# A selective-scan kernel: the middle row group interleaved by padded weights, one DMA per quad, pieces at other units, and states that enter a scan through its first token

## The chip, the cores and the metric

The kernel runs on one core of a Trainium2 chip. The metric is the device time of one execution in microseconds (us), from three runs. Before the change it is 13006.98 us at the median (13003.53 to 13008.28). Profiles are of one execution; their times count from the first instruction. The engines are TensorE (PE, with its weight loads as PEld), VectorE (DVE), ScalarE (ACT), GpSimd (POOL) and SyncE (SP), which issues the DMAs here. Each works through its own queue in order.

## The reference

The input is x of shape (2, 96, 128, 128) in float32. The model has two layers, and nearly all of the time goes into the first half of the first one: four Mamba blocks that read the normalized image as a sequence of 16384 tokens in four directions (rows, rows reversed, columns, columns reversed). Each block has 192 inner channels and 16 states per channel.

```python
xc, z = jnp.split(x @ in_w.T, 2, axis=-1)          # 96 -> 192 and 192
xc = silu(causal_conv4(xc) + conv_b)               # depthwise, 4 taps
xdbl = xc @ xproj_w.T                              # dt_raw (6), B (16), C (16)
dt = softplus(dt_raw @ dt_w.T + dt_b)
h = exp(dt * A) * h + dt * B * u                   # for each token, channel, state
y = einsum('bds,bs->bd', h, C)
y = (y + Dp * xc) * silu(z)
out = y @ outp_w.T                                 # then the fuse over 4 directions
```

After the Mamba blocks come a quantized feed-forward layer, a 3x3 convolution and a second feed-forward layer, with normalizations between. The change does not touch these.

## The kernel before

For each of the two images the kernel runs three stages one after the other: normalize (the image by rows and by columns goes to DRAM), mamba, and ffn_and_conv. Only mamba and the weights' setup change.

**Tiling.** Directions are worked on in pairs (PAIRS): a row direction and a column direction, 2 x 192 = 384 channels, in three groups g of 128 partitions. Group 0 holds channels 0 to 127 of the first direction, group 2 the last 128 of the second, and the middle group, g = 1, holds 64 of each: partitions 0 to 63 for the first direction, 64 to 127 for the second. A *step* is 512 tokens of one pair; there are 32 steps in a pair and 64 in an image. Step i = 0 of a pair starts from zero states. Within a step the states of a group are taken two at a time. Such a pair of states of one group is a *unit*: 24 units in a step, units 0 to 7 of group 0, 8 to 15 of group 1, 16 to 23 of group 2.

**A unit's work.** ACT computes the decay exp(dt * A) for the two states into PSUM (`decay`, L330). POOL multiplies the B rows by dt * u (`b_part`, L324). DVE runs two scans over the 512 tokens (`scan`, L334), one for each state, with the recurrence's multiply and add in one instruction, and then multiplies the states by the C rows (L409). PE adds these products into the output y by matmuls with the identity (`sums`, L341). ACT copies the last states into `hst` (L410); the scan of the same unit in the next step takes them as its initial value. When a group's eight units are done, DVE multiplies y with the gate (`gated`, L349), PE starts the next group's y with the skip term (L416), and `project` and `collect` bring two groups at a time into the result (L357 to L365).

**Rows.** B and C are the same for all channels of a direction, so each step writes its 64 rows to DRAM in four copies (`rows_out`, L261, four DMAs) and reads them back onto 128 partitions, four states at once, a *quad* of 1 MB that serves two units (`row_tile`, L320). For the middle group a quad comes by two DMAs, each to 64 partitions.

**Order.** All engine queues are written out by hand. The loop runs over the units of all steps. In unit k it issues, in this order: the fetch of a B quad (every second unit, for unit k + 6), POOL's `b_part` for unit k + 2, pieces due at (k, 0), the first scan of unit k, everything behind unit k - 1 (product, state copy, gated product, sums), the second scan of unit k, the fetch of a C quad (for k + 4), ACT's decay for unit k + 2, and pieces due at (k, 1).

**Pieces.** The next step's input work is spread over the units of this one, at the places in the table `at` (L301 to L310): loading the input (`load`), three convolutions (`conv`, `conv_out`; the four taps are folded into the weights, L207 and L233), three gate projections (`gate`, `gate_out`), two `silu` passes with a table load before and after (L244, L245), the projection to B, C and dt (`rows`, `rows_out`), and for each group seven pieces that make dt by a softplus (`dt_in` on PE; `dt_exp`, `dt_ln` on ACT; `dt_q`, `dt_log`, `dt_sum`, `dt_u` on POOL). Convolutions, gates, rows, dt_in and project share one PSUM buffer, `misc`, so that each waits until ACT has read the one before. For the middle group `inproj` issues, for each tap, two matmuls of 64 output rows, one from each direction.

**Setup.** Weights are loaded once; the convolution's input weights are multiplied by their taps (L97), and the output projection is folded with the fuse weights into `gmat` (L112).

Of the kernel before, what the change touches and what calls it, by code (L numbers as in the profile page):

```python
# [42 lines left out]
def tile_metaformer(ctx: ExitStack, tc: tile.TileContext, a: dict, out: bass.AP):  # L43
# [22 lines left out]
    inz = const("inz", (C, 4, DI))  # L66
# [11 lines left out]
    inx = cpool.tile([C, 4, 4, DI], F32, name="inx")  # L78
    nc.vector.memset(gmat, 0.0)
    with tc.tile_pool(name="prep", bufs=1) as pp, tc.tile_pool(name="prep_ps", bufs=2, space=PSUM) as pps:  # L80
# [11 lines left out]
        inxw = pp.tile([C, 4, DI], F32, name="inxw")  # L92
        nc.sync.dma_start(inxw, a["inx"])
        taps = pp.tile([C, 4, 4, DI], F32, name="taps")
        nc.sync.dma_start(taps, a["taps"].broadcast_to((C, 4, 4, DI)))
        for d in range(4):
            nc.vector.tensor_tensor(inx[:, d], taps[:, d], inxw[:, d, None, :].broadcast_to((C, 4, DI)), ALU.mult)  # L97
        outw = pp.tile([C, 4, DI], F32, name="outw")
        nc.sync.dma_start(outw, a["outw"])
        fusew = pp.tile([C, 4, C], F32, name="fusew")  # L100
        nc.sync.dma_start(fusew, a["fusew"])
        for pi, (da, db) in enumerate(PAIRS):

            pieces = [
                (slice(0, 128), da, 0, 128),
                (slice(0, 64), da, 128, 192),
                (slice(64, 128), db, 0, 64),
                (slice(0, 128), db, 64, 192),
            ]
            for g, (rows, d, lo, hi) in enumerate(pieces):  # L110
                ps = pps.tile([128, C], F32, name="ps")
                nc.tensor.matmul(ps[rows, :], outw[:, d, lo:hi], fusew[:, d, :], start=True, stop=True)  # L112
                nc.vector.tensor_copy(gmat[rows, pi, g, :], ps[rows, :])
# [69 lines left out]
    def mamba(acc, xnr, xnc):  # L183

        with ExitStack() as st:
# [5 lines left out]
            hst = one.tile([128, NG, S], F32, name="hst")  # L191
            acc_w = acc.rearrange("c (h w) -> c w h", w=W)
# [4 lines left out]
            def inproj(pi, g, w, src, taps):  # L197

                ps = misc()
                for k in taps:  # L200
                    se = {"start": k == taps[0], "stop": k == taps[-1]}
                    for d, rows, lo, hi in (
                        ((0, slice(0, 128), 0, 128),),
                        ((0, slice(0, 64), 128, 192), (1, slice(64, 128), 0, 64)),
                        ((1, slice(0, 128), 64, 192),),
                    )[g]:
                        nc.tensor.matmul(ps[rows, :], w(PAIRS[pi][d], k, lo, hi), src[d][:, k : k + T], **se)  # L207
                return ps

            def prologue(pi, i, d):  # L210
# [16 lines left out]
                def conv(g):  # L227
                    d["ps"] = inproj(pi, g, lambda dd, k, lo, hi: inx[:, dd, k, lo:hi], src, (0, 1, 2, 3))
# [6 lines left out]
                def gate(g):  # L235
                    d["ps"] = inproj(pi, g, lambda dd, k, lo, hi: inz[:, dd, lo:hi], src, (3,))
# [18 lines left out]
                def rows_out():  # L255

                    d["rows"] = one.tile([BCO + NBC, T], F32, name="rows")
                    nc.scalar.copy(d["rows"], d["ps"][0 : BCO + NBC, :])
                    d["bcd"] = rows_d.tile([COPIES, 2, NBC // 2, T], F32, name="bcd")
                    for n in range(COPIES):  # L260
                        nc.sync.dma_start(d["bcd"][n].rearrange("k r t -> (k r) t"), d["rows"][BCO:, :])  # L261
# [38 lines left out]

                at = [(0, 0, load), (8, 1, partial(silu, "xc")), (14, 1, partial(silu, "sz"))]  # L301
                at += [(12, 0, rows), (12, 1, rows_out)]
                for g, k in enumerate((4, 5, 6)):
                    at += [(k, 0, partial(conv, g)), (k, 1, partial(conv_out, g))]
                for g, k in enumerate((7, 10, 11)):
                    at += [(k, 0, partial(gate, g)), (k, 1, partial(gate_out, g))]
# [129 lines left out]
            for k in range(total + 6):  # L436
# [4 lines left out]
                if k % 2 == 0:  # L441
                    fetch(k + 2 * B_AHEAD, 0, B_AHEAD, bs)
# [180 lines left out]
```

## Time and profile before

| What | Value |
|---|---|
| Time, median of three runs | 13006.98 us |
| Profiled execution | 13004.29 us |
| Its span, first to last instruction | 13002.5 us |
| DVE busy | 11569.1 us, 89% |
| PE busy | 10850.3 us, 83% |
| POOL busy | 9215.4 us, 71% |
| ACT busy | 8560.0 us, 66% |
| DMA queue q1, share of 16 engines | 83.1%, 3394.12 MB |
| POOL's waits for rows (L324) | 1419.2 us |
| DVE's waits for rows (L409) | 18.8 us |
| Mean granted TensorE clock | 0.963 |

Busy time is the union of an engine's instructions. A group is a set of instructions with the same line, engine, operation and tiles; its row gives the busy time, the mean duration in ns, and the idle time of the engine just before these instructions with what ended it. Instructions of DVE and POOL overlap a little at their ends, so that their pitch, from start to start, is shorter than their duration. In a timeline a row begins with its start and its length in us; a bracket gives the idle time before it and who ended it.

The two mamba stages are the stretches in which DVE is at 90% or more: from 168 to 5937 us, and from 6661 to 12427 us.

### The profile page before, as it was taken

The numbers are of one execution on the slowest core, as the hardware profiler recorded it, in microseconds if no ns is written. First come the engines' busy times: TensorE is split into PE (matmuls) and PEld (weight loads), VectorE is DVE, ScalarE is ACT, GpSimd is POOL, SyncE is SP. The second block draws the span as 40 slices with busy tenths as digits, with TensorE's granted clock in tenths as the row PEclk, the third lists the DMA queues.
The fourth block names the chain that finished last, engine by engine and source line by source line (L and its number), as shares of the span: only waits on it lengthen the run. The fifth ranks groups of instructions, "written<-read, shape, count | busy, mean of one in ns | idle before, by whom it ended". The sixth has DMA issues, their size and how long they took to land. (4 is left out here: it accounts for less than half of the span.)

```text
span 13002.5 us, 97992 instructions
## 1 busy us (share of the span) xinstructions
PE 10850.3 (83%) x24208; PEld 3987.1 (31%) x24208; DVE 11569.1 (89%) x10865; ACT 8560.0 (66%) x14738; POOL 9215.4 (71%) x4772
## 2 busy tenths in 40 slices
PE   6888888888888888888978888888888888888889
PEld 2323233333333333333323333332333333333233
DVE  5999999999999999995459999999999999999954
ACT  6666666666666666665566666666666666666655
POOL 4877778777787787772147778777787777877721
PEclk8999999999999999999989999999999999999999
DMA  7999999999999999992079999999999999999920
GB/s 226 287 294 282 298 288 285 295 283 298 288 285 295 283 295 289 285 295 68 13 226 285 298 283 292 290 285 298 285 291 291 284 298 286 290 294 281 296 61 13
DMA packets 545331, 3400.40 MB, mean 262 GB/s; under 512 B 81612, under 2 KB 82732, under 8 KB 146840
## 3 DMA queue, kind: packets, MB, share of 16 engines
q1 hardware_dynamic: 544760, 3394.12, 83.1%
q8 instruction: 195, 3.19, 0.1%
q14 instruction: 376, 3.08, 0.1%
HBM read 3288.94 MB, written 104.86 MB: 261 GB/s over the span
## 5 line engine op out<-in xcount | busy, mean ns | idle before, releaser
L324 POOL TENSOR_TENSOR row<-dtu,row 128x1024 f32<-128x1024 f32 x3072 | 7175.7, 2358 | 1739.3 <-DMA row<-bcd 1419.2
L334 DVE TENSOR_TENSOR_SCAN da<-da,hst,row 128x512 f32<-128x512 f32 x5952 | 7339.4, 1274 | 351.2 <-ACT da L330 194.6
L341 PE MATMUL y<-row,ident 128*128 128x512 f32 x12288 | 6120.1, 626 | 1113.3 <-DVE row L409 1098.9
L330 ACT ACTIVATE da<-dt,amat 128x512 f32<-128x512 f32 x6144 | 4249.4, 692 | 207.5 <-ACT hst L410 0.4
L341 PEld LDWEIGHTS y<-row,ident 128*128 128x128 f32 x12288 | 2288.9, 197 | 4779.4 <-DVE row L409 2292.3
L409 DVE TENSOR_TENSOR row<-da,row 128x1024 f32<-128x1024 f32 x3072 | 3705.9, 1206 | 19.6 <-DMA row<-bcd 18.8
L410 ACT COPY hst<-da 128x2 f32<-128x2 f32 x3072 | 484.0, 158 | 2235.5 <-DVE row L409 2233.3
L416 PE MATMUL y<-xc,dmat 128*128 128x512 f32 x768 | 526.1, 773 | 779.1 <-DVE sz L349 779.1
L287 POOL TENSOR_TENSOR q<-e,q 128x512 f32<-128x512 f32 x384 | 488.0, 1271 | 821.8 <-ACT hst L410 709.1
L233 ACT ACTIVATE xc<-misc,convb 128x512 f32<-128x512 f32 x384 | 264.2, 688 | 1117.5 <-PE misc L207 1117.5
L207 PE MATMUL misc<-xa,inx 96*128 96x512 f32 (+1 forms) x2048 | 932.4, 597 | 59.0 <-DMA xa<-xnr 57.2
L207 PE MATMUL misc<-xb,inx 96*64 96x512 f32 (+1 forms) x2048 | 928.1, 595 | 1.6 <-ACT xc L233 1.6
L531 POOL TENSOR_TENSOR acc<-acc,y 96x512 f32<-96x512 f32 x128 | 147.6, 1153 | 987.0 <-DVE y L530 987.0
L541 PE MATMUL pc<-pad,kw 96*96 96x512 f32 x1152 | 566.7, 593 | 0.0
L207 PEld LDWEIGHTS misc<-xa,inx 96*128 96x128 f32 (+1 forms) x2048 | 323.6, 163 | 625.5 <-issue 493.4
L293 POOL TENSOR_TENSOR dt<-dt,ln 128x512 f32<-128x512 f32 x384 | 486.9, 1268 | 30.1
L297 POOL TENSOR_TENSOR dtu<-dt,xc 128x512 f32<-128x512 f32 x384 | 488.5, 1272 | 0.5
L290 POOL TENSOR_TENSOR ln<-ln,q 128x512 f32<-128x512 f32 x384 | 488.1, 1271 | 0.5
L359 PE MATMUL misc<-sz,gmat 128*96 128x512 f32 x1024 | 483.6, 594 | 0.0
L416 PEld LDWEIGHTS y<-xc,dmat 128*128 128x128 f32 x768 | 129.0, 211 | 1102.1 <-DVE sz L349 1099.1
L268 PE MATMUL misc<-rows,dtw 12*128 12x512 f32 x768 | 439.7, 652 | 18.5 <-ACT dt L275 17.2
L132 DVE TENSOR_TENSOR xq<-xm,rs 96x512 fp8e5<-96x512 f32 x128 | 87.9, 687 | 387.8 <-ACT rs L128 387.8
(75 smaller groups left out, 8403.8 us busy)
## 6 DMA issues: line engine op xcount, KB each, us to landing
row<-bcd SPq DMA_DIRECT2D x2048, 1024.0 KB, 7.5
row<-bcd SPq DMA_DIRECT2D x2048, 512.0 KB, 8.0
bcd<-rows SPq DMA_DIRECT2D x512, 128.0 KB, 9.8
xa<-xnr SPq DMA_DIRECT2D x124, 193.1 KB, 5.8
xb<-xnc SPq DMA_DIRECT2D x124, 193.1 KB, 5.5
acc<-in_x_dram SPq DMA_DIRECT2D x16, 768.0 KB, 17.8
xnr<-xn SPq DMA_DIRECT2D x16, 768.0 KB, 4.3
xnc<-stg SPq DMA_DIRECT2D x16, 768.0 KB, 5.6
```

The source lines that it names most:

```text
L207: nc.tensor.matmul(ps[rows, :], w(PAIRS[pi][d], k, lo, hi), src[d][:, k : k + T], **se)
L287: nc.gpsimd.tensor_tensor(d["q"], d["e"], d["q"], ALU.subtract)
L290: nc.gpsimd.tensor_tensor(d["ln"], d["ln"], d["q"], ALU.add)
L293: nc.gpsimd.tensor_tensor(d["dt"][g], d["dt"][g], d["ln"], ALU.add)
L297: nc.gpsimd.tensor_tensor(dtu, d["dt"][g], d["xc"][:, g, :], ALU.mult)
L324: nc.gpsimd.tensor_tensor(b, d["dtu"][g][:, None, :].broadcast_to((128, 2, T)), b, ALU.mult)
L330: nc.scalar.activation(da[:, j, :], d["dt"][g], AF.Exp, scale=amat[:, pi, g, s + j : s + j + 1])
L334: nc.vector.tensor_tensor_scan(h[:, j, :], da[:, j, :], b[:, j, :], 0.0 if i == 0 else hst[:, g, s + j : s + j + 1], ALU.mult, ALU.add,)
L341: nc.tensor.matmul(y, ident, c[:, j, :], start=False, stop=s + j == S - 1)
L409: nc.vector.tensor_tensor(c, h, c, ALU.mult)
L416: nc.tensor.matmul(y, dmat[:, pi, g, :], d["xc"][:, g, :], start=True, stop=False)
L541: nc.tensor.matmul(pc, kw[:, t, :], rows, start=t == 0, stop=t == 8)
```

## The change

1. **States through the first token.** A scan's initial value is the constant 0.0. Instead, the state that enters a step is added to the first token's input: for each group ACT computes exp(dt * A) of the step's first token (128x16) and POOL multiplies it by `hst` into `enter` (`entering`, due at units 20, 28 and 36 counted from the start of the step before), and in every unit of a step with i > 0 POOL adds two columns of `enter` to the first token of the B product.
2. **The middle group's rows in turn.** Its 128 channels alternate between the two directions, partition by partition. Setup pads the weights with zero columns (`padded`), so that each of the middle group's matmuls has 128 output columns, half of them zero, and both directions accumulate into the same PSUM rows: eight matmuls in a row for a convolution, two for a gate.
3. **One DMA per quad.** With channels in turn, the copies in DRAM are laid out so that one DMA fills 128 partitions for the middle group too. The copies are written by two DMAs with a broadcast instead of four.
4. **Pieces at other units.** The table `at` changes; outputs are now one unit after the matmuls they read. Writing the rows to DRAM is a piece of its own.
5. **Setup.** The taps are loaded in four parts through one buffer, and `gmat` needs no clearing.

```diff
             hst = one.tile([128, NG, S], F32, name="hst")
+            enter = one.tile([128, NG, S], F32, name="enter")
...
-            def inproj(pi, g, w, src, taps):
+            def inproj(g, w, src, taps):
 
                 ps = misc()
-                for k in taps:
-                    se = {"start": k == taps[0], "stop": k == taps[-1]}
-                    for d, rows, lo, hi in (
-                        ((0, slice(0, 128), 0, 128),),
-                        ((0, slice(0, 64), 128, 192), (1, slice(64, 128), 0, 64)),
-                        ((1, slice(0, 128), 64, 192),),
-                    )[g]:
-                        nc.tensor.matmul(ps[rows, :], w(PAIRS[pi][d], k, lo, hi), src[d][:, k : k + T], **se)
+                parts = [(k, j) for k in taps for j in ((0,), (1, 2), (3,))[g]]
+                for n, (k, j) in enumerate(parts):
+                    nc.tensor.matmul(ps, w(k, j), src[j // 2][:, k : k + T], start=n == 0, stop=n == len(parts) - 1)
                 return ps
...
                 def rows_out():
-
                     d["rows"] = one.tile([BCO + NBC, T], F32, name="rows")
                     nc.scalar.copy(d["rows"], d["ps"][0 : BCO + NBC, :])
-                    d["bcd"] = rows_d.tile([COPIES, 2, NBC // 2, T], F32, name="bcd")
-                    for n in range(COPIES):
-                        nc.sync.dma_start(d["bcd"][n].rearrange("k r t -> (k r) t"), d["rows"][BCO:, :])
+
+                def rows_to_dram():
+
+                    d["bcd"] = rows_d.tile([2, COPIES, NBC // 2, T], F32, name="bcd")
+                    for k in range(2):
+                        r = d["rows"][BCO + k * NBC // 2 : BCO + (k + 1) * NBC // 2, None, :]
+                        r = r.broadcast_to((NBC // 2, COPIES, T))
+                        nc.sync.dma_start(d["bcd"][k].rearrange("n r t -> r n t"), r)
...
-                at = [(0, 0, load), (8, 1, partial(silu, "xc")), (14, 1, partial(silu, "sz"))]
-                at += [(12, 0, rows), (12, 1, rows_out)]
-                for g, k in enumerate((4, 5, 6)):
-                    at += [(k, 0, partial(conv, g)), (k, 1, partial(conv_out, g))]
-                for g, k in enumerate((7, 10, 11)):
-                    at += [(k, 0, partial(gate, g)), (k, 1, partial(gate_out, g))]
-                for g, k in enumerate((13, 18, 21)):
-                    pieces = (0, 0, dt_in), (0, 1, dt_exp), (1, 1, dt_ln), (2, 0, dt_q), (3, 0, dt_log), (3, 0, dt_sum), (4, 0, dt_u)
+                at = [(0, 0, load), (7, 1, partial(silu, "xc")), (12, 1, partial(silu, "sz"))]
+                at += [(12, 1, rows), (13, 0, rows_out), (13, 1, rows_to_dram)]
+                for g, k in enumerate((2, 4, 6)):
+                    at += [(k, 0, partial(conv, g)), (k + 1, 0, partial(conv_out, g))]
+                for g, k in enumerate((9, 10, 11)):
+                    at += [(k, 1, partial(gate, g)), (k + 1, 0, partial(gate_out, g))]
+                for g, k in enumerate((14, 17, 20)):
+                    pieces = (0, 1, dt_in), (1, 0, dt_exp), (1, 1, dt_ln), (3, 0, dt_q), (4, 0, dt_log), (4, 0, dt_sum), (5, 0, dt_u)
                     at += [(k + m, where, partial(f, g)) for m, where, f in pieces]
...
-                for half in range(2) if g == 1 else (slice(None),):
-                    rows = slice(half * 64, half * 64 + 64) if g == 1 else half
-                    at = s + S * (half if g == 1 else g // 2)
-                    n = (64 if g == 1 else 128) // COPIES
-                    src = d["bcd"][None, :, k, at : at + 4, :].broadcast_to((n, COPIES, 4, T))
-                    nc.sync.dma_start(t[rows], src)
+
+                rows, nd = d["bcd"][k].rearrange("n (d s) t -> n d s t", d=2)[:, :, s : s + 4, :], 2
+                if g != 1:
+                    rows, nd = rows[:, g // 2 : g // 2 + 1], 1
+                src = rows.rearrange("n d s t -> (n d) s t")[None].broadcast_to((128 // nd // COPIES, nd * COPIES, 4, T))
+                nc.sync.dma_start(t, src)
                 return t
 
-            def b_part(d, g, b):
+            def entering(pi, d, g):
+
+                nc.scalar.activation(enter[:, g, :], amat[:, pi, g, :], AF.Exp, scale=d["dt"][g][:, 0:1])
+                nc.gpsimd.tensor_tensor(enter[:, g, :], enter[:, g, :], hst[:, g, :], ALU.mult)
+
+            def b_part(i, d, g, s, b):
                 nc.gpsimd.tensor_tensor(b, d["dtu"][g][:, None, :].broadcast_to((128, 2, T)), b, ALU.mult)
+                if i > 0:
+                    nc.gpsimd.tensor_tensor(b[:, :, 0], b[:, :, 0], enter[:, g, s : s + 2], ALU.add)
...
-            def scan(i, g, s, j, da, b, h):
-                nc.vector.tensor_tensor_scan(
-                    h[:, j, :], da[:, j, :], b[:, j, :],
-                    0.0 if i == 0 else hst[:, g, s + j : s + j + 1], ALU.mult, ALU.add,
-                )
+            def scan(j, da, b, h):
+                nc.vector.tensor_tensor_scan(h[:, j, :], da[:, j, :], b[:, j, :], 0.0, ALU.mult, ALU.add)
...
+                    if steps[n + 1][1] > 0:
+                        for g in range(NG):
+                            later(k + nu - 4 + nu // NG * g, 1, entering, steps[n + 1][0], state[n + 1], g)
...
+    def padded(w):
+
+        t = np.zeros((w.shape[0], 2, NG + 1, 128), f)
+        for pi, (p, q) in enumerate(PAIRS):
+            t[:, pi, 0] = w[:, p, :128]
+            t[:, pi, 1, 0::2] = w[:, p, 128:]
+            t[:, pi, 2, 1::2] = w[:, q, :64]
+            t[:, pi, 3] = w[:, q, 64:]
+        return t
```

## The prediction

> **What bounds the kernel now.** I read the busy shares first (page, part 1), then the groups by shape, then one steady step of the scan stage in each engine's timeline, then stretches of 3 us for DMA and clock. VectorE (DVE) is busy for 89% of the span. Its rows, and GpSimd's (POOL) product, as groups by shape:
>
> ```profile
> L334 DVE TENSOR_TENSOR_SCAN da<-da,hst,row 128x512 f32<-128x512 f32 x5952 | 7339.4, 1274 | 351.2 <-ACT da L330 194.6 <-ACT hst L410 134.2 <-issue 21.2
> L334 DVE TENSOR_TENSOR_SCAN da<-da,row 128x512 f32<-128x512 f32 x192 | 225.6, 1214 | 180.9 <-POOL row L324 170.9 <-ACT hst L410 5.2 <-ACT da L330 4.7
> L324 POOL TENSOR_TENSOR row<-dtu,row 128x1024 f32<-128x1024 f32 x3072 | 7175.7, 2358 | 1739.3 <-DMA row<-bcd 1419.2 <-DVE row L409 256.6 <-DVE da L334 63.4
> ```
>
> The 192 scans of the first steps (i = 0) start from the constant 0.0, as all scans of the changed kernel will. DVE's timeline gives the pitch of a unit (two scans, one product) from start to start, with states and from zero:
>
> ```profile
> 2013.07 2.45 DVE L334 TENSOR_TENSOR_SCAN da<-da,hst,row 128x512 f32<-128x512 f32 x2
> 2015.43 1.21 DVE L409 TENSOR_TENSOR row<-da,row 128x1024 f32<-128x1024 f32 x1
> 2016.56 2.45 DVE L334 TENSOR_TENSOR_SCAN da<-da,hst,row 128x512 f32<-128x512 f32 x2
> ...
> 179.60 2.33 DVE L334 TENSOR_TENSOR_SCAN da<-da,row 128x512 f32<-128x512 f32 x2
> 181.84 1.21 DVE L409 TENSOR_TENSOR row<-da,row 128x1024 f32<-128x1024 f32 x1
> 182.97 2.33 DVE L334 TENSOR_TENSOR_SCAN da<-da,row 128x512 f32<-128x512 f32 x2
> ```
>
> 3.487 us against 3.365 us. With three gated products (0.595 us of pitch each) a step without a wait takes 24 x 3.487 + 1.8 = 85.5 us. Scans at the same place follow each other after 89.88 us (2001.76, 2091.63, 2181.52), so 4.4 us are waits, at three fixed places: scan of unit 9, gated product in unit 9, scan of unit 17. DVE, then TensorE (PE), then ScalarE (ACT) show why:
>
> ```profile
> 2091.63 1.29 DVE L334 TENSOR_TENSOR_SCAN da<-da,hst,row 128x512 f32<-128x512 f32 x1 [1.49 <-ACT da L330]
> 2095.37 0.69 DVE L349 TENSOR_TENSOR sz<-y,sz 128x512 f32<-128x512 f32 x1 [1.33 <-PE y L341]
> ```
> ```profile
> 2075.06 3.60 PE L207 MATMUL misc<-xa,inx 96*128 96x512 f32 x8
> ...
> 2080.30 0.64 PE L207 MATMUL misc<-xa,inx 96*64 96x512 f32 x1
> 2080.31 0.64 PE L207 MATMUL misc<-xb,inx 96*64 96x512 f32 x1
> ...
> 2083.89 1.98 PE L341 MATMUL y<-row,ident 128*128 128x512 f32 x4
> ```
> ```profile
> 2089.35 0.69 ACT L233 ACTIVATE xc<-misc,convb 128x512 f32<-128x512 f32 x1 [3.15 <-PE misc L207]
> 2090.12 1.41 ACT L330 ACTIVATE da<-dt,amat 128x512 f32<-128x512 f32 x2
> ```
>
> ACT's queue is in order: it sits 3.15 us on a convolution that PE has not finished, the decay for unit 9 stands behind it, and DVE waits for that decay. In units 3 to 8 PE has more work than the units have time. Last, DMA and the TensorE clock (last three columns: clock, DMA share, GB/s):
>
> ```profile
> 1975.00:1978.00 3.00, 3.00 (x6) 1.04 (x5) 3.00 (x4) 0.57 (x2) 3.00 (x3) 0.53 0.96 309
> ...
> 2099.00:2102.00 3.00, 3.00 (x9) 0.91 (x10) 3.00 (x4) 2.70 (x6) 0.00 (x0) 1.00 1.04 235
> ...
> 2120.00:2123.00 3.00, 1.98 (x4) 0.68 (x4) 1.73 (x3) 2.87 (x7) 1.59 (x2) 1.00 1.04 437
> ```
>
> The half quads of the middle group move 235 GB/s at full share, whole quads 437.
>
> [...] The xa and xb matmuls of 64 columns start 10 ns apart[...]. [...] The trace shows 0.53 after a PE gap of only 2.1 us. [...]L293 behind L290 starts 1.35 us after it where others take 1.22, so a wait costs 0.13 us.
>
> **The change part by part**, per step, for the 124 steps with i > 0.
>
> *States through the first token.* DVE: 24 x (3.487 - 3.365) = -2.9 us. POOL gets 24 adds of 128x2 and three small products. From pitches of 2.31 us (1024) and 1.22 (512) a tiny operation is 0.13 us, with its wait 0.26; bounds 0.15 and 0.5. POOL goes from 24 x 2.31 + 12 x 1.22 = 70 us to 77. ACT's three exponentials of 128x16 (0.2 us each, near the 0.158 of L410) lie in its idle time, except that POOL waits for the one at unit 20.
>
> *One DMA per quad.* 8.4 MB at 235 GB/s become 8.4 MB at about 430: 36 us of transfers become 20. DVE's product waited for rows only 18.8 us in all, POOL's 1419 us of such waits end elsewhere: gain 0 to 20 us in all, taken as 10. Two bcd DMAs for four carry the same bytes, issued a unit later on SP; units 18 to 24 cover it.
>
> *Padded weights.* Convolution g = 1 has eight matmuls of 128 columns in turn: 8 x 0.86 = 6.9 us where four pairs took 3.5. Its gate takes 1.72 for 0.86, at units 9 to 11 where PE has room.
>
> *Pieces moved.* Convolutions run in units 2, 4, 6 instead of 4, 5, 6. I follow PE from the gated product in unit 1 (time 0), by pitches of this step: dmat and sums(0) end at 3.4, conv 0 at 6.9, sums(1) 8.6, project (L357 reads with a stride: 3.44) 12.0, sums(2) 13.7, conv 1 20.6. ACT copies it (0.6), then state copy and decay for unit 7: done at 23.0. DVE without waits wants unit 7 at 1.7 + 5 x 3.365 = 18.5: a wait of 4.6 us. On: sums(3), sums(4), conv 2 end at 27.5, its copy and the decay for unit 9 at 29.9, silu with two table loads (4.09) 34.0, decay for unit 10 at 35.6. Unit 10 was due at 29.2: 6.5 us lost, where the step of before loses 1.6 + 1.4 = 3.0 (a resumed DVE loses 0.1 beyond the idle shown). So +3.5. Silu of sz no longer shares a unit with the logarithm: the wait at unit 17 (1.4) goes; silu plus rows (4.8 us behind the decay for unit 14) leave about 0.5 at unit 15: -0.9.
>
> *What queues behind PE.* SP fetches C rows into a buffer that sums(3) frees: at 22.3, and with the median 7.5 us to landing they are there at 29.9, wanted by the product of unit 8 at 31; the B fetch behind it on SP is wanted later still. +0, with 1 us of cover.
>
> *POOL's lateness.* From the gated product in unit 17: PE 3.4 and dt_in 1.1; ACT dt_exp 1.7, dt_ln 2.0, collect 0.6, three state copies with decays 4.6, the exponential 0.2; POOL its product 0.3, feeds 23 to 25 at 2.57 each, logarithm, sum and dtu 3.8. Together 25.4 (25.7 with the latencies between), and DVE wants b(25) at 1.7 + 7 x 3.365 = 25.3: +0.3. Feeds 27 and 28 come up to 2 us late, but DVE then waits for unit 7 anyway.
>
> *Clock.* In some 4 of 10 steps of before the light stretch ahead of unit 1 halves the clock (the 0.53 line); these steps take 90.66 us, 0.78 more, after 0.65 us of PE idle absorbed part of it. The changed queue has no such idle: about 1.5 us instead, and behind the same gap ahead of unit 17 stands dt_in(1), whose decay for unit 20 has 0.8 us of slack. Estimate +0.6, bounds 0 and +1.2.
>
> Sum: -2.9 + 3.5 - 0.9 + 0.3 + 0.6 = +0.6 us a step, 124 steps: +75. Once: setup reloads taps four times through one buffer (+6), two serial first prologues (+9), first steps with the longer conv (+10), DMA -10: +15. The profiled execution (13004.3, span 13002.5) becomes 13094; the median shown is 2.7 higher. I take 13100.
>
> **Rivals.** *Tie:* PE's loss as worked out, but POOL in time and the clock no worse: 0.9 less a step, 12985 to 13030. For it: the sum without estimates is -0.3 a step. *Faster:* PE's extra 3.4 us does not delay ACT, because conv 1 finds a gap: waits stay at 3.0 + 0.5, step 86.4, 12540; halfway 12800. Against it: PE shows no gap from 2065 to 2095. It decides if conv 1 ends before time 16. *Much slower:* POOL's small add costs 0.5 us, not 0.13: three adds lie between unit 20's exponential and b(25), over 1 us more, then every feed is late: 13300. It decides from about 0.2 us, since no slack is left at b(25). For it: POOL at 77 of 82.6 us. *The change misses its aim* (scans stay at 1.18): the i = 0 rows speak against it.
>
> **How the numbers follow.** Forecast 0.50 (own range 13035 to 13190), tie 0.20, faster 0.20, much slower 0.10. About 0.2% (26 us) is what this measurement can tell. Slower: 0.45 of the forecast and the 0.10, 0.55; within: 0.05 of the forecast and 0.13 of the tie; faster: the other 0.07 of the tie and 0.20. The range, 12860 to 13290, leaves out most of faster (0.12) and half of much slower (0.05).
>
> **What would show it.** Scans of 1.21 us with a unit pitch of 3.365; DVE's longest wait for ACT's decay at unit 7, ACT's for PE at conv 1; PE's x8 row taking 6.9 us for g = 1; no wait at unit 17; DMA share near 0.7. Wrong if conv 1 takes 3.5 us, if unit 7 waits under 3 us, or if DVE waits longer for POOL than for ACT.

## The result and the profile after

The changed kernel takes 13457.52 us at the median (13442.77 to 13467.8), the kernel before 13007.63 us beside it (13003.53 to 13014.97). The ratio is 1.0344, with a 95% interval of 1.0326 to 1.0362: slower by 3.4%, some 450 us. The forecast was 13100 us, with a range of 12860 to 13290.

The groups of the page after, the same rows as were shown of before, and GpSimd's new small add (columns as there: busy time, mean ns of one, idle time before it and what ended most of it):

```profile
L322 POOL TENSOR_TENSOR row<-dtu,row 128x1024 f32<-128x1024 f32 x3072 | 7230.8, 2354 | 1929.5 <-DMA row<-bcd 1555.2
L334 DVE TENSOR_TENSOR_SCAN da<-da,row 128x512 f32<-128x512 f32 x6144 | 7273.2, 1218 | 983.6 <-ACT hst L407 368.8
...
L406 DVE TENSOR_TENSOR row<-da,row 128x1024 f32<-128x1024 f32 x3072 | 3716.1, 1210 | 403.6 <-DMA row<-bcd 394.2
...
L324 POOL TENSOR_TENSOR row<-row,enter 128x2 f32<-128x2 f32 x2976 | 576.7, 194 | 233.4
```

The scans run from zero at the forecast 1.21 to 1.22 us, and the small add costs 0.19 us. New is the third row: VectorE's product waits 394.2 us for rows, where before it waited 18.8. Two lines of the page's DMA parts say that the rows did not come faster:

```profile
q1 hardware_dynamic: 524616, 3394.73, 80.7%
...
row<-bcd SPq DMA_DIRECT2D x3072, 1024.0 KB, 9.3
```

The same lines of before, whole quads and halves apart:

```profile
q1 hardware_dynamic: 544760, 3394.12, 83.1%
...
row<-bcd SPq DMA_DIRECT2D x2048, 1024.0 KB, 7.5
row<-bcd SPq DMA_DIRECT2D x2048, 512.0 KB, 8.0
```

The share of the 16 DMA engines was to fall to about 0.70; it is 80.7% (83.1% before), and a quad takes 9.3 us to land (7.5 us for whole quads, 8.0 for halves before). Stretches of 3 us of one step, with clock, DMA share and GB/s as the last three columns:

```profile
2069.00:2072.00 3.00, 3.00 (x8) 1.32 (x7) 1.58 (x2) 1.31 (x3) 2.92 (x3) 1.00 0.00 0
...
2084.00:2087.00 3.00, 3.00 (x8) 1.10 (x6) 1.98 (x3) 2.86 (x5) 2.83 (x3) 1.00 1.01 218
2114.00:2117.00 3.00, 2.84 (x7) 1.13 (x7) 3.00 (x4) 1.17 (x2) 3.00 (x2) 1.00 1.04 431
```

The middle group's quads now fill 128 partitions with one DMA, and still move 218 GB/s at full share; those of the other groups move 431. And from 2069 to 2072 us the DMA engines stand idle, because SyncE, which works through its fetches in order, waits for a C buffer: in the stretch from 2062 to 2076 us its own waits show 9.6 us for TensorE's sums, in one piece. VectorE's timeline of the same step shows what comes of it:

```profile
2066.00 2.33 DVE L334 TENSOR_TENSOR_SCAN da<-da,row 128x512 f32<-128x512 f32 x2
2068.24 1.21 DVE L406 TENSOR_TENSOR row<-da,row 128x1024 f32<-128x1024 f32 x1
2069.36 1.22 DVE L334 TENSOR_TENSOR_SCAN da<-da,row 128x512 f32<-128x512 f32 x1
2072.95 1.23 DVE L334 TENSOR_TENSOR_SCAN da<-da,row 128x512 f32<-128x512 f32 x1 [2.37 <-ACT hst L407]
...
2098.21 1.23 DVE L406 TENSOR_TENSOR row<-da,row 128x1024 f32<-128x1024 f32 x1 [1.36 <-DMA row<-bcd]
```

From 2066.00 to 2069.36 is one unit without a wait: the pitch of 3.365 us that was forecast. The wait of 2.37 us is at unit 7, where it was expected; the one of 1.36 us at the product in unit 13 was not. (A product is issued one unit late: the one in unit 13 belongs to unit 12. Products are named here by the unit in which they run.) TensorE and ScalarE ahead of unit 7:

```profile
2063.59 1.02 PE L196 MATMUL misc<-xa,inx 96*128 96x512 f32 x2
...
2069.60 1.02 PE L196 MATMUL misc<-xb,inx 96*128 96x512 f32 x2
2070.46 3.60 PE L338 MATMUL y<-row,ident 128*128 128x512 f32 x8
```
```profile
2070.66 0.69 ACT L222 ACTIVATE xc<-misc,convb 128x512 f32<-128x512 f32 x1 [5.83 <-PE misc L196]
...
2072.97 1.42 ACT L330 ACTIVATE da<-dt,amat 128x512 f32<-128x512 f32 x2
```

The middle group's convolution takes from 2063.59 to 2070.46, 6.9 us; ScalarE sits on it for 5.83 us, with the decays behind. While it runs, the sums that free C buffers wait too: SyncE's waits for TensorE are 5121.6 us in all (4676.5 before), the longest 12.0 us (8.1).

Summed over 118 steady steps of each trace, VectorE's waits by place, in us a step (0.1 us and more counted; "32 x 4" is the first experiment below):

| Wait of VectorE | before | after | 32 x 4 |
|---|---|---|---|
| scans of units 0, 3, 4 (for GpSimd, in the main) | 0 | 0.39, 1.50, 0.33 | 0.31, 1.50, 0.32 |
| scan of unit 7 (for ScalarE) | 0 | 2.95 | 3.05 |
| scans of units 8, 9 (that of 9 for ScalarE) | 0.18, 1.60 | 0 | 0 |
| gated product in unit 9, scan of unit 10 | 1.32, 0 | 0.51, 1.02 | 0.52, 1.01 |
| products in units 13, 15 (for rows) | 0, 0.15 | 2.22, 1.02 | 0, 0 |
| scans of units 15, 17, 20 | 0, 1.10, 0 | 0, 0, 0.24 | 0.41, 0, 0.42 |
| all | 4.36 | 10.23 | 7.53 |
| step, scan to scan | 90.24 | 93.92 | 91.16 |

The step is 3.7 us longer; over 124 steps that is 456 of the 463 us between the two profiled executions (13467.8 and 13004.3). 3.2 us of the waits are for rows.

### The profile page after: what moved, and what is told of

The parts are those of the page before. It is cut to its first block, busy times and chain, and to the rows that moved or that the text cites. A ratio compares the mean times of both kernels' runs of the same rounds, so it can differ in the third digit from the quotient of the medians.

```text
span 13466.0 us, 99149 instructions
## 1 busy us (share of the span) xinstructions
PE 11209.5 (83%) x24208; PEld 4303.5 (32%) x24208; DVE 11297.8 (84%) x10864; ACT 8633.9 (64%) x15110; POOL 9844.4 (73%) x8120
## 3 DMA queue, kind: packets, MB, share of 16 engines
q1 hardware_dynamic: 524616, 3394.73, 80.7%
## 5 line engine op out<-in xcount | busy, mean ns | idle before, releaser
L334 DVE TENSOR_TENSOR_SCAN da<-da,row 128x512 f32<-128x512 f32 x6144 | 7273.2, 1218 | 983.6 <-ACT hst L407 368.8
L406 DVE TENSOR_TENSOR row<-da,row 128x1024 f32<-128x1024 f32 x3072 | 3716.1, 1210 | 403.6 <-DMA row<-bcd 394.2
L196 PE MATMUL misc<-xa,inx 96*128 96x512 f32 x2048 | 998.4, 599 | 60.6 <-DMA xnc<-stg 57.5
L196 PE MATMUL misc<-xb,inx 96*128 96x512 f32 x2048 | 983.5, 592 | 1.6 <-ACT xc L222 1.6
L413 PE MATMUL y<-xc,dmat 128*128 128x512 f32 x768 | 447.9, 666 | 581.0 <-DVE sz L346 581.0
L324 POOL TENSOR_TENSOR row<-row,enter 128x2 f32<-128x2 f32 x2976 | 576.7, 194 | 233.4
L266 ACT ACTIVATE e<-misc,dtb 128x512 f32<-128x512 f32 x384 | 264.1, 688 | 636.4 <-PE misc L261 587.0
L196 PEld LDWEIGHTS misc<-xa,inx 96*128 96x128 f32 x2048 | 399.0, 195 | 583.7 <-issue 544.0
L196 PEld LDWEIGHTS misc<-xb,inx 96*128 96x128 f32 x2048 | 386.5, 189 | 494.7 <-issue 491.2
```

The costliest lines, as they stand in the source:

```text
L196: nc.tensor.matmul(ps, w(k, j), src[j // 2][:, k : k + T], start=n == 0, stop=n == len(parts) - 1)
L324: nc.gpsimd.tensor_tensor(b[:, :, 0], b[:, :, 0], enter[:, g, s : s + 2], ALU.add)
L334: nc.vector.tensor_tensor_scan(h[:, j, :], da[:, j, :], b[:, j, :], 0.0, ALU.mult, ALU.add)
L406: nc.vector.tensor_tensor(c, h, c, ALU.mult)
```

## The experiments

### The middle group's source as 32 x 4

```diff
-                src = rows.rearrange("n d s t -> (n d) s t")[None].broadcast_to((128 // nd // COPIES, nd * COPIES, 4, T))
+                if g == 1:
+                    rows = rows[0:2]
+                src = rows.rearrange("n d s t -> (n d) s t")[None].broadcast_to((32, 4, 4, T))
```

The other groups' source already is 32 x 4 and stays. The middle group uses two of its four copies.

> The changed kernel with one line different: the middle group's source is written as 32 repetitions of 4 chunks (two copies times two directions) in place of 16 repetitions of 8 chunks. The values read and the bytes are the same. Rate theory: the middle quads ran at 218 GB/s [...] not because of the partitions they fill; with 32 x 4 they run at about 430 as the other groups' do, the products of units 13 and 15 stop waiting for rows (394 us in the page falls under 60), the DMA share falls to about 0.70, and the time is the one after less 3.2 to 3.5 us a step: 13020, 12970 to 13110. Lateness theory: the C fetches come late because TensorE frees the C buffers late, whatever the rate: the waits at 13 and 15 stay above 2 us a step together, and the time above 13300.

Measured: 13127.56 us (13116.36 to 13133.96), ratio to before 1.0094 (1.0079 to 1.0109). From the page's DMA part and VectorE's groups (all that ended the idle time, not only most of it):

```profile
q1 hardware_dynamic: 524616, 3394.73, 69.5%
```
```profile
L408 DVE TENSOR_TENSOR row<-da,row 128x1024 f32<-128x1024 f32 x3072 | 3712.8, 1209 | 0.1
```

One line takes 330 us away. The share falls to 69.5%, the product's waits for rows from 394 us to nothing. So the rate theory holds, and TensorE's lateness alone is not enough for a wait. The time is above the 13110 that was given; the step is 91.16 us. What the prediction worked out for the kernel with fast rows, 13094 for the profiled execution, is 13116 here.

### Source patterns or places

```diff
-                src = rows.rearrange("n d s t -> (n d) s t")[None].broadcast_to((128 // nd // COPIES, nd * COPIES, 4, T))
+                src = d["bcd"][k][0, 0:4, :]
+                copy = NBC // 2 * T
+                pattern = ([T // 2, 16], [copy // 2, 8]), ([T // 2, 32], [copy, 4]), ([T // 4, 64], [copy, 2])
+                src = bass.AP(tensor=src.tensor, offset=src.offset, ap=[*pattern[g], [1, 4 * T]])
```

> The changed kernel with other source patterns for the quads, so that B and C are other rows than they should be; bytes, destinations and chunk sizes are kept. In every group the 128 partitions read 128 different (overlapping) places: group 0 as 16 x 8, the middle group as 32 x 4, the last group as 64 x 2. Split theory: what counts is the source's outermost count; group 0 falls to about 218 GB/s (8 KB packets of about 620 ns), the middle and the last group run at about 430 (about 309 ns). Source theory: what counts is how many different places in DRAM are read; all three groups run at one rate, 218 or less. Time theory: the middle group's stretch is slow because of what else runs then; it stays at 218 and the other two at 430.

Measured: 14543.76 us, one run; why it is slower than the changed kernel by so much was not followed. The first two of these 3 us stretches fall on the middle and the last group's quads, the last one on group 0's:

```profile
2054.00:2057.00 3.00, 2.21 (x6) 1.04 (x6) 3.00 (x3) 2.18 (x5) 2.47 (x2) 1.00 1.03 429
2075.00:2078.00 3.00, 1.98 (x4) 0.68 (x4) 3.00 (x4) 2.87 (x6) 2.92 (x3) 1.00 1.00 415
...
2102.00:2105.00 3.00, 1.34 (x3) 0.68 (x4) 3.00 (x4) 1.99 (x4) 2.92 (x4) 1.00 1.01 224
```

A quad is 128 packets of 8 KB. In the order of the queue, the trace's packet records give the time of a packet in each quad; the medians over the quads of the first image, in ns, good to some 1%:

| Kernel | group 0 | middle group | group 2 |
|---|---|---|---|
| before (whole, two halves of 16 x 4, whole) | 309 | 612 | 312 |
| after (32 x 4, 16 x 8, 32 x 4) | 309 | 610 | 312 |
| middle group as 32 x 4 | 309 | 309 | 309 |
| this one (16 x 8, 32 x 4, 64 x 2) | 606 | 309 | 309 |
| halves of 32 x 2 (last experiment) | 309 | 619 | 312 |

Among whole quads the slow group is the one whose source has 16 as its outermost count (606 and 610 ns, against 309 to 312), wherever in the step it is fetched, and although in this run all groups read 128 different places. The split theory holds, the other two fall. (To 128 partitions 16 always comes with an inner count of 8, so these runs can't tell the two counts apart.)

### States through the first token, alone

```diff
+            def entering(pi, d, g):
+                nc.scalar.activation(enter[:, g, :], amat[:, pi, g, :], AF.Exp, scale=d["dt"][g][:, 0:1])
+                nc.gpsimd.tensor_tensor(enter[:, g, :], enter[:, g, :], hst[:, g, :], ALU.mult)
...
+                if i > 0:
+                    nc.gpsimd.tensor_tensor(b[:, :, 0], b[:, :, 0], enter[:, g, s : s + 2], ALU.add)
...
-                    0.0 if i == 0 else hst[:, g, s + j : s + j + 1], ALU.mult, ALU.add,
+                    0.0, ALU.mult, ALU.add,
```

> The kernel before with the first part of the change alone (states enter through the first token); layout, DMAs and table as before. By the prediction's terms: scans save 2.9 us a step, of which about 0.9 is lost again ahead of unit 9, where TensorE sets the time, and about 0.3 at GpSimd's lateness: 1.3 to 1.9 us a step, 12770 to 12840. If GpSimd's 24 small adds are what made the change slower, this kernel is slower than before, 13100 or more. If the row transfers already bind the kernel before (half-rate quads), what DVE gains returns as waits for rows at the products of the middle group, and the time stays within 0.5% of before.

Measured: 13071.44 us, ratio 1.0052 (1.0035 to 1.0069): slightly slower. The time lies just outside the 0.5% of the third expectation, but not for its reason, since the waits for rows grow only from 0.15 to 0.53 us a step; the reason is the second's, GpSimd, short of its 13100. VectorE's scans as a group:

```profile
L342 DVE TENSOR_TENSOR_SCAN da<-da,row 128x512 f32<-128x512 f32 x6144 | 7285.5, 1218 | 818.7 <-POOL row L332 391.3
```

VectorE's waits grow from 4.36 to 7.06 us a step, which takes back 2.7 of the 2.9 that the scans give: 2.8 us of new waits at units 0, 1, 3 and 4, behind GpSimd's small add (L332), while only 0.7 goes at units 8 to 10. The step is still longer, 90.77 against 90.24: VectorE now waits 8.5 times a step where it waited 3.7 times, and loses some 0.1 us beyond the idle time at each (without the waits counted, the step is 83.7 us where the pitches say 82.6; before, 85.9 and 85.5). Whether the clock takes part can't be told: of the 29 steady steps of the first pair in the first image, 28 have a stretch in which TensorE's granted clock is halved, 3.4 us or more (25 before, at a granted clock of 0.50; 19 in the 32 x 4 kernel), so that there is next to nothing to compare with. The part is no gain in this order of the work.

### Without half of the middle convolution

```diff
-                parts = [(k, j) for k in taps for j in ((0,), (1, 2), (3,))[g]]
+                parts = [(k, j) for k in taps for j in ((0,), (1, 2) if len(taps) == 1 else (1,), (3,))[g]]
```

> The changed kernel without the second direction's four matmuls in the middle group's convolution, so that half of that group's channels get only their bias there: TensorE's work at that place is 3.4 us instead of 6.9. TensorE/ScalarE window: the wait at unit 7 falls from 2.9 us to under 0.5, so up to 3 us a step. If the row waits at units 13 and 15 come from TensorE's lateness in freeing C buffers, they go too, and the time is about 12650 to 12750. If they come from the rate of the middle quads, they stay or grow by what unit 7 gives up, and the time is above 13000 (13050 to 13400).

Measured: 13043.84 us, one run, just under the 13050 that was given. The wait at unit 7 falls from 2.95 to 0.19 us a step; the row waits at 13 and 15 stay, 2.20 and 1.18. So TensorE's burst makes the wait at unit 7, and not those for rows.

The same edit on the 32 x 4 kernel prices the convolution without them:

> The changed kernel with the 32 x 4 source, and without the second direction's four matmuls in the middle group's convolution (half of that group's channels get only their bias there). With rows no longer late, this prices the padded convolution alone. Window theory (the term of +3.5 us a step in the prediction): the wait at unit 7 falls from 3.05 us to under 0.4 and the step from 91.1 to 88.0 to 88.6 us, 12730 to 12810 in all. Rival: GpSimd's lateness takes the place of that wait (unit 3 already waits 1.5 us for it), the step stays above 90 us, 13000 or more.

Measured: 12686.56 us, ratio to before 0.9758 (0.9739 to 0.9778), 441 us below the 32 x 4 kernel, a little more than expected. The step is 87.9 us, and the wait at unit 7 falls from 3.05 to 0.24. GpSimd's waits at units 0, 3 and 4 stay at 2.1 us and do not grow. Four matmuls of 0.86 us, 3.4 us of TensorE, cost 3.3 us of step.

### Without the entering states

```diff
-                if i > 0:
-                    nc.gpsimd.tensor_tensor(b[:, :, 0], b[:, :, 0], enter[:, g, s : s + 2], ALU.add)
...
-                            later(k + nu - 4 + nu // NG * g, 1, entering, steps[n + 1][0], state[n + 1], g)
```

> The changed kernel with the 32 x 4 source, and without the states that enter a step: every step starts from zero, with no exponential of 128x16, no product with the last states and no add of two columns. This prices the work on GpSimd that replaces the scans' initial values. Absorption theory (as the prediction has it): the waits for GpSimd at units 0, 3 and 4, 2.1 us together, go, and the wait at unit 7 grows by nearly as much, because TensorE's convolutions set that time; the step falls by 0.2 to 0.9 us, 13010 to 13100. Rival: GpSimd's lateness is on the path by itself; the step falls by 2 us or more, 12870 or less.

Measured: 12984.45 us, 143 us or 1.1 us a step below the 32 x 4 kernel, between the two expectations and nearer to absorption. The waits at units 0, 3 and 4 (2.1 us) go, and the wait at unit 7 grows from 3.05 to 4.54. One such step in VectorE's timeline:

```profile
2079.23 1.23 DVE L334 TENSOR_TENSOR_SCAN da<-da,row 128x512 f32<-128x512 f32 x1 [4.79 <-ACT hst L407]
```

So 1.5 of 2.1 us were hidden by TensorE's window. Most of the gain lies in units 13 to 25, which take 0.9 us less, and two things make it. Where the clock is not halved there, these units take 41.9 us with the entering states and 41.3 without. And fewer steps have a halved stretch at all, 6 of 29 against 19; that part comes by the clock. Whole steps without one take 89.95 and 89.27 us.

### The old table of pieces

```diff
-                at = [(0, 0, load), (7, 1, partial(silu, "xc")), (12, 1, partial(silu, "sz"))]
+                at = [(0, 0, load), (8, 1, partial(silu, "xc")), (14, 1, partial(silu, "sz"))]
...
-                for g, k in enumerate((2, 4, 6)):
-                    at += [(k, 0, partial(conv, g)), (k + 1, 0, partial(conv_out, g))]
+                for g, k in enumerate((4, 5, 6)):
+                    at += [(k, 0, partial(conv, g)), (k, 1, partial(conv_out, g))]
...
-                for g, k in enumerate((14, 17, 20)):
+                for g, k in enumerate((13, 18, 21)):
```

> The changed kernel with the 32 x 4 source and the table of pieces of before: convolutions at units 4, 5 and 6 with their copies in the same unit, silu of sz at unit 14, dt at 13, 18 and 21. This prices the moved pieces alone. The prediction's term: TensorE's chain of work from unit 1 to the last convolution is the same in either table, so the window costs about the same, and the waits at units 15 to 17 that the new table takes away (0.9 us a step) come back: 0.5 to 1.5 us a step slower than with the new table, 13190 to 13310. Rival: the new places cost more than they save, because ScalarE waits for the long convolution two units earlier; then the old table is faster, 13000 or less.

Measured: 13462.17 us, ratio 1.0351 (1.0335 to 1.0366): 335 us slower than the 32 x 4 kernel with the new table, of the expected sign, but almost twice the most that was expected. The waits at units 8 and 9 are 5.4 us together, and the one at unit 17 is back (1.52). All 29 steady steps of that first pair have a halved stretch of the clock, where the new table leaves ten free. The new places are the best part of the change, worth 2.7 us a step where the padded convolution has to be done.

### Spread: a version against the waits

The 32 x 4 kernel, with the convolutions in parts of one or two taps, the first of them already in unit 21 of the step before; GpSimd's product three units ahead (FEED) instead of two; and the entering product apart from its exponential.

```diff
-                at = [(0, 0, load), (7, 1, partial(silu, "xc")), (12, 1, partial(silu, "sz"))]
-                at += [(12, 1, rows), (13, 0, rows_out), (13, 1, rows_to_dram)]
+                at = [(-6, 0, load), (7, 1, partial(silu, "xc")), (12, 1, partial(silu, "sz"))]
+                at += [(11, 1, rows), (12, 0, rows_out), (12, 1, rows_to_dram)]
+                halves = (0, 1), (2, 3)
+                for g, k, parts in ((0, -3, halves), (1, -1, ((0,), (1,), (2,), (3,))), (2, 5, halves)):
+                    at += [(k + m, 1, partial(conv, g, taps)) for m, taps in enumerate(parts)]
+                    at += [(k + len(parts), 0, partial(conv_out, g))]
...
+                    for g, (exp, mul) in enumerate(((18, 20), (23, 26), (30, 33))):
+                        later(k + exp, 1, entering, steps[n + 1][0], state[n + 1], g)
+                        later(k + mul, 0, entering_state, g)
...
-                feed(k + AHEAD)
+                feed(k + FEED)
```

> A version meant to be better than both kernels: the changed kernel with the 32 x 4 source, the convolutions spread in two, four and two parts from unit 21 of the step before to unit 6, the pieces of dt one to a unit and those of the last group after the step's end, GpSimd's product three units ahead in place of two, and the entering states' product two or three units behind their exponential. If TensorE's burst ahead of unit 9 and GpSimd's queue behind the exponentials are what the waits of units 0 to 10 are made of, these waits fall from 8 us to 1 to 3 us a step, the step to 84.5 to 86.5 us, and the time to 12290 to 12560. If another limit stands close behind (ScalarE at 67 us of work a step in another order, or rows late again), the step stays above 88 us, 12750 or more.

Measured: 12814.03 us, ratio 0.9856 (0.984 to 0.9873): faster than before, and short of what was expected. No wait is left at units 3, 4 and 7. Others took their place, in us a step: 1.62 at unit 10, 1.33 at 15, 1.05 at 20, 0.57 at 1. At 10 and 15 ScalarE's silu, 4.1 us with its two table loads, stands in or next to a unit with another piece for ScalarE. All 29 steps of the first pair have a halved stretch of the clock, some of 10.2 us.

### Spread, second version

The edit is shown against the first spread version.

```diff
-                at = [(-6, 0, load), (7, 1, partial(silu, "xc")), (12, 1, partial(silu, "sz"))]
-                at += [(11, 1, rows), (12, 0, rows_out), (12, 1, rows_to_dram)]
+                at = [(-7, 0, load), (7, 0, partial(silu, "xc")), (18, 0, partial(silu, "sz"))]
+                at += [(7, 1, rows), (8, 1, rows_out), (8, 1, rows_to_dram)]
...
-                for g, k in enumerate((8, 9, 10)):
-                    at += [(k, 1, partial(gate, g)), (k + 1, 0, partial(gate_out, g))]
+                for g, k, o in ((0, 11, (12, 0)), (1, 14, (15, 0)), (2, 16, (17, 0))):
+                    at += [(k, 1, partial(gate, g)), (*o, partial(gate_out, g))]
...
-                    ((13, 1), (14, 0), (14, 1), (15, 0), (16, 0), (17, 0), (18, 0)),
-                    ((17, 1), (18, 0), (19, 0), (20, 0), (21, 0), (22, 0), (24, 0)),
-                    ((20, 0), (21, 1), (23, 0), (26, 0), (27, 0), (29, 0), (31, 0)),
+                    ((8, 1), (9, 1), (10, 1), (12, 0), (13, 0), (14, 0), (15, 0)),
+                    ((12, 1), (13, 1), (16, 0), (18, 0), (19, 0), (20, 0), (22, 0)),
+                    ((20, 0), (21, 0), (22, 1), (24, 0), (26, 0), (28, 0), (30, 0)),
...
```

> The spread version with the remaining waits taken one by one: both silu passes (4.1 us with their table loads) in units of their own, ScalarE's copies out of PSUM behind the unit's decay, the gates at units 11, 14 and 16 so that TensorE does not fall idle ahead of unit 17, the second projection at unit 9. If the waits at units 10 and 15 (1.6 and 1.3 us) came from silu together with another piece in one unit, and those at 1 and 20 from the halved clock, they go, the step falls from 88.7 to 84.5 to 86.5 us, and the time to 12300 to 12560. If ScalarE's silu costs a wait wherever it stands, 2 us a step stay and the time is 12600 or more.

Measured: 12038.25 us (12037.17 to 12039.15), ratio 0.9256 (0.924 to 0.9271), better than expected. The page's first part, and VectorE's scans:

```profile
PE 10849.8 (90%) x24208; PEld 4273.4 (36%) x24208; DVE 11154.0 (93%) x10864; ACT 8648.5 (72%) x15110; POOL 9830.6 (82%) x8120
```
```profile
L346 DVE TENSOR_TENSOR_SCAN da<-da,row 128x512 f32<-128x512 f32 x6144 | 7169.9, 1213 | 172.5 <-POOL row L334 172.4
```

In the 118 steady steps no wait of 0.1 us is left. The step is 82.55 us, the 24 x 3.365 + 1.8 = 82.6 that VectorE needs without any wait. The 172 us are outside these steps. The steady steps have no stretch of halved clock. So, with fast quads, each of the padded layout's costs can be hidden; what the 32 x 4 kernel still pays is the order.

### The second version with 16 x 8

The source line of the first experiment is put back, nothing else.

> The second spread version with the changed kernel's own source pattern for the middle group, 16 x 8, and nothing else different. The row DMAs then need about 39 us of transfer for 16 quads at 430 GB/s and 38.5 us for 8 at 218, with the rest of the DMAs some 83 us a step, against a step of 82.55 us. If that rate binds, the waits for rows come back whatever the order of the pieces, the step is 86 to 92 us, 12450 to 13200 in all. If it only bit because TensorE freed the C buffers late, it is hidden here, and the time stays under 12150.

Measured: 12563.75 us, ratio 0.9663 (0.9635 to 0.9692). VectorE's product in the groups:

```profile
L416 DVE TENSOR_TENSOR row<-da,row 128x1024 f32<-128x1024 f32 x3072 | 3703.2, 1205 | 465.0 <-DMA row<-bcd 461.2 <-PE misc L197 3.2
```

The step is 86.7 us, 4.1 more, with waits of 0.65 us at the product in unit 13 and 2.91 in 15. TensorE's convolutions are in parts here, and the same order with 32 x 4 waits for nothing. So the rate binds by itself at this pace, as the estimate of 83 us of transfers against a step of 82.55 said.

### The second version with states in the scans

```diff
-                if i > 0:
-                    nc.gpsimd.tensor_tensor(b[:, :, 0], b[:, :, 0], enter[:, g, s : s + 2], ALU.add)
...
-                nc.vector.tensor_tensor_scan(h[:, j, :], da[:, j, :], b[:, j, :], 0.0, ALU.mult, ALU.add)
+                nc.vector.tensor_tensor_scan(
+                    h[:, j, :], da[:, j, :], b[:, j, :],
+                    0.0 if i == 0 else hst[:, g, s + j : s + j + 1], ALU.mult, ALU.add,
+                )
```

> The second spread version with the last states as the scans' initial value, as in the kernel before, and without GpSimd's and ScalarE's work for the first token. This is the price of the change's first part where no engine but VectorE binds. By the pitches of 3.487 and 3.365 us the step is 24 x 3.487 + 1.8 = 85.5 us, 2.9 more: 12370 to 12430. If the first-token work costs VectorE nothing but gains nothing either, within 50 us of 12038.

Measured: 12398.73 us, ratio 0.9537 (0.9509 to 0.9564). The step is 85.47 us, again without a wait: 2.92 more, where the two pitches say 24 x 0.122 = 2.93.

### Halves of 32 x 2

```diff
                     src = d["bcd"][None, :, k, at : at + 4, :].broadcast_to((n, COPIES, 4, T))
+                    if g == 1:
+                        src = d["bcd"][None, 0:2, k, at : at + 4, :].broadcast_to((32, 2, 4, T))
```

> The kernel before with one line different: each half quad of the middle group, 64 partitions, reads its source as 32 repetitions of 2 copies in place of 16 of 4. [...] the halves stay at 218 to 240 GB/s with 8 KB packets of about 620 ns, the DMA share stays at 82 to 83%, and the time within 0.2% of before, 12975 to 13030. Source theory: the halves were slow for the same reason as the 16 x 8 quads; they run at about 430, the DMA share falls to about 70%, and the few waits for rows go: 12900 to 12990.

Measured: 13070.55 us, ratio 1.0056 (1.004 to 1.0073). A stretch in the middle group's transfers:

```profile
2093.00:2096.00 3.00, 3.00 (x8) 1.32 (x8) 3.00 (x4) 1.12 (x2) 3.00 (x2) 1.00 1.03 218
```

The halves stay at 218 GB/s and 619 ns a packet, so the source theory falls: the halves are slow with a source of 32 x 2 as with one of 16 x 4 (612 ns). That 64 partitions make it, and not something else of the halves, no run tested alone. The kernel is a little slower where nothing was expected: the product in unit 15 waits 0.78 us a step (0.15 before). Reading two copies in place of four is the only edit; why it costs that was not followed.

## Why the prediction was right and wrong

The direction was right, the time 2.7% too low, and outside its range. Point by point, by its own steps:

- **One DMA per quad: the step that failed.** "8.4 MB at 235 GB/s become 8.4 MB at about 430" did not happen: 610 ns a packet after, 612 before. The prediction saw that halves are slow, and took it that one DMA to 128 partitions would be as fast as the whole quads of the trace: the author's estimate, not shown. The halves are slow with another source too (619 ns, last experiment). But the same edit gave the middle group a source of 16 x 8, where the only whole pattern of the trace is 32 x 4; the trace of before does not show 16 x 8, and it is as slow as the halves though it fills 128 partitions. An unseen pattern was to be bounded from both sides; "gain 0 to 20 us" left out that the quads stay slow and what is late then.
- **"+0, with 1 us of cover" for the C rows** failed with it, though not at the quad for which it was worked out: unit 8's lands 1.4 us ahead of its product on average, and no wait is there. It stopped at that quad. At 218 GB/s a quad takes 4.8 us, they queue behind one another, and in the stretch from 2076 to 2090 us they took 14.5 us to land, where the prediction used the median of 7.5 us, that of whole, fast quads. The quads of units 12 and 14 land 2.2 and 0.9 us late; with 32 x 4 they are 7.4 and 8.8 us early (averages over the steady steps whose landings the trace tells). Together these two steps cost 330 us, 2.7 us a step (93.92 against 91.16). The rate is the cause: with fast quads TensorE's lateness makes no wait, and with slow ones the waits stay when half a convolution is left out, and come back in the second spread version. That the kernel before, with the same rate, waits only 0.15 us a step is a narrow escape: these two quads land 1.2 and 0.5 us ahead of their products there. The first part of the change alone makes the wait in unit 15 0.53, two copies for four 0.78. Which of the other edits used up the rest was not separated.
- **PE/ACT window, +3.5: right.** The prediction had 6.5 us lost up to unit 10, of which 4.6 at unit 7. With fast rows the waits of units 0 to 10 sum to 6.7; without GpSimd's part they are 6.4, with 4.54 at unit 7. Half a convolution less gives 3.3 us back.
- **Scans from zero, -2.9: right,** 2.92 where nothing else binds.
- **Silu and the wait at unit 17, -0.9: nearly right.** 1.10 at unit 17 becomes 0.41 at unit 15, -0.7. The whole move of the table was worth more, 2.7 us a step, against the old table with the padded convolution, a case that the prediction did not price.
- **GpSimd's lateness, +0.3:** too small. Without it the step is 1.1 us shorter, 0.7 in steps of undisturbed clock and the rest by the clock. The late feeds at units 3 and 4, and that most of their waits is absorbed at unit 7, were right. The rival *much slower* set its limit at about 0.2 us for the small add; it took 0.19.
- **Clock, +0.6:** about +0.9. With fast rows a step free of halved stretches takes 89.95 us and most others 91.65, and the mean of 91.16 is 1.2 above the clean one; before has 0.36 (90.24 and 89.88). That the clean steps are so alike, 89.95 and 89.88, says that the terms other than clock and rows, which the prediction summed to 0.0, do come to nothing.
- **A reading that was wrong, without effect.** Against *faster* the prediction says that TensorE shows no gap from 2065 to 2095. It has one, the 0.65 us ahead of 2068.08 that the clock term counts.
- **"Would show" and "wrong if".** Scan time, pitch, the place of the wait, 6.9 us and no wait at unit 17 were seen; the DMA share near 0.7 was the one that was not, and it is the failed step. The wait at unit 7, 2.95 us, is under the 3 that was given as a sign of error, since GpSimd's waits at units 0 to 4 take a part of it ahead.

The kernel that the prediction had in mind, with quads that are fast, was run: 13127.56 us against 13100. Part of this nearness is luck. The terms of GpSimd and of the clock were too small by some 0.3 to 0.4 us a step each, and others must have come out lower, since the step grew by 0.92 us where 0.6 was forecast. The one-time +15 was not seen: 124 steps of 0.92 us more already make 114 us, and the profiled executions (13116.36 and 13004.29) differ by 112.

Why 16 x 8 is slow is not settled: the runs show the rate of each pattern, and not what makes it. Measured are about 606 to 610 ns a packet for 16 x 8, and 309 for 32 x 4 and 64 x 2.

## What to carry to other kernels

When an edit replaces a slow transfer pattern, look for the new pattern itself, source and destination, in the trace; if it isn't there, price the case that it is as slow as the old one, and follow who then is late. A saving on the busiest engine (2.9 us a step here) is worth nothing while other engines' bursts set its waits: the same part cost 0.5% in the old order and gave 2.9% in a good one (12398.73 to 12038.25). Spread long pieces into parts no longer than the slack of a unit, keep two long pieces of one engine in different units, and put the consumer of a small result some units behind its producer: that took the 32 x 4 kernel's 91.16 us a step to VectorE's own 82.55.

## What the runs showed that was not expected

- A DMA of 1 MB to 128 partitions runs at half rate, 218 GB/s in place of 430, when its source is written as 16 x 8 chunks of 8 KB, and at full rate as 32 x 4 or 64 x 2.
- A source of two copies in place of four for the 64-partition halves left the packets at 619 ns (612 before), and yet the kernel took 0.56% longer.
- In the second spread version there was no halved stretch of TensorE's clock in the steady steps of either mamba stage, 5.3 ms each, and the mean over the run rose to 0.99 (0.963 before). The first spread version had one in each of the 29 steps of the first pair, and the second with 16 x 8 in 21 of them. What decides it was not worked out.
